# Seven block products with four shared sums, all on DVE, in a two-layer decoder on one core; norms by halves, a reordered start

## The chip, the cores and the metric

The kernel runs on one NeuronCore of a Trainium2 chip. The metric is device time in microseconds, from launch to end, as the median of several executions. PE is the matrix engine (TensorE), PEld its weight loads, DVE the VectorE, ACT the ScalarE, POOL the GpSimd engine and SP the SyncE, which here only issues transfers. All data are float32.

## What is computed

The input x holds 16 sequences of 128 tokens, 256 features each. It goes through two decoder layers of three parts; each part's output is added to x and the sum is layer-normed:

```python
x = layernorm(x + L0_attn(x))      # causal, 16 heads of 64
x = layernorm(x + L0_xattn(x))     # 8 experts of 512, relu, gated by token ids and ctx
x = layernorm(x + L0_ffn(x))       # 2 shared and 16 routed experts, top 2, silu
x = layernorm(x + L1_attn(x))      # 16 heads of 16, a band of 8 tokens to each side
x = layernorm(x + L1_xattn(x))     # 16 heads of 16, keys and values from ctx
x = layernorm(x + L1_ffn(x))       # 8 experts of 512, gelu, all of them, one factor per token
```

The two parts with eight dense experts (the second and the sixth) need, for every expert, `h = act(x @ up)` (512 wide) and `h @ down` (back to 256), summed over the experts.

## The kernel before

**Tiling.** The 16 sequences are four groups of four, 512 tokens each. A group's x stays in SBUF as 128 tokens by 4 sequences by 256 features, and its transpose xT as 2 x 128 features by 512 tokens. There are six parts for each of four groups, so 24 pieces of work, `run(number, g)`.

**Order of the work.** `Weaver` (from L196) is a planner inside the kernel: every part is a generator that emits instructions and yields how many microseconds of PE they are thought to take, or a time until which it wants to wait. `weave` takes pieces from a main stream (attention parts) and a side stream (`dense`: the expert parts) in given shares, and from short streams first (transposes, norms' tails, gates). At first only attention of groups 0 and 1 runs; then attention of groups 2 and 3 beside the dense parts of the first groups, and so on; the last group's sixth part runs alone at the end. The framework then orders each engine's instructions once more by a plan of its own, so the order in the built program differs from that of emission. Each engine's queue is worked off in order. An instruction that waits holds up all behind it on its engine.

**The start.** `load_x(0)`, the first quad of attention weights (four transfers of 256 KB: W_Q, W_K, W_V, W_O for four heads), then x of the other three groups (L106 to L108), all on SP's queue. Four streams `tail(-1, g)` transpose all groups' x (L51, copied by L244 and L246), and the first of them also starts `gates0`, which selects by token id in the transferred `it` and `cx` (L743, tile chose).

**attention0** (L347) goes through four quads of four heads. `project_quad` makes q and k (L288, drained by L361 and L366) and v (L305, L309); per quad and sequence follow scores (L382), mask, maximum and exponential (L319, L324, L329), the scaling of e by 1/sum on POOL (L335), its transpose (L51, drained by L344), the values (L424) and the output projection (L391). The next quad's projections are spread over the current quad's four sequences; the last quad has none to spread.

**products** (L640) does `h @ down` for an expert by Strassen's seven products of 2 x 2 blocks: tokens are halved, and h's features are halved. Of h, five sums of two blocks are needed (L663): three go to DVE and two to POOL, in tiles cm. Of the weights, seven combinations are made once on POOL (L629 to L631), used and written to HBM, from where later groups load them. The seven products of an expert are four calls of `multiply`, two products each (one in the last), in PSUM banks M of which there are two; DVE adds each bank to acc in SBUF (L681). After the eighth expert, `products_end` forms the four blocks of the result from the seven accumulated products with eight sums (L709 to L716, six on DVE and two on POOL, tile y), transposes them (L51), and adds them to x (L264 or L266). `Norm.done` (L274) then makes 1/sqrt(variance + eps) of four sequences, with the power on POOL (L278), and scales x (L280). For the last part, `store` writes a group's 512 KB of x out (L966). The hidden activations are drained by L774 (DVE, second part) or L933 (ACT, sixth part).

Of the kernel before, what the change touches and what calls it, by code (L numbers as in the profile page):

```python
# [8 lines left out]
F32 = mybir.dt.float32  # L9
# [18 lines left out]
def kernel(ctx: ExitStack, tc: tile.TileContext, a: dict, out: bass.AP):  # L28
# [77 lines left out]
    xs = [load_x(0)]  # L106
    first_quad = load_quad(0)
    xs += [load_x(g) for g in range(1, NG)]  # L108
# [5 lines left out]
    nc.gpsimd.memset(ones, 1.0)  # L114
    mhalf = cp.tile([P, GB], F32, tag="mhalf", name="mhalf")
# [133 lines left out]
    class Norm:  # L249
# [24 lines left out]
        def done(self):  # L274
            ve = sp.tile([P, GB], F32, tag="ve", name="ve")
            nc.vector.tensor_scalar(ve, self.mv[:, :, 1], EPS, None, ALU.add)
            rstd = sp.tile([P, GB], F32, tag="rstd", name="rstd")
            nc.gpsimd.tensor_tensor(rstd, ve, mhalf, ALU.pow)  # L278
            for b in range(GB):
                nc.vector.tensor_scalar(  # L280
                    self.x[:, b, :], self.x[:, b, :],
                    self.mv[:, b, 0:1], rstd[:, b:b + 1], ALU.subtract, ALU.mult,
                )
# [63 lines left out]
    def attention0(x, xT, g):  # L347
        norm = Norm(x)
        norm.bias(bo0)
        heads = {}  # L350

        def project_quad(j):
            wq, wk, wv, wo = first_quad if g == 0 and j == 0 else load_quad(j)
# [16 lines left out]
            heads[j] = qT, kT, v, wo  # L370

        def scores(j, b):
            qT, kT, _, _ = heads[j]
# [14 lines left out]
        def output(j, b, zT):  # L388
            po = bank("H")[:, :D]
            for i in range(2):  # L390
                mm(po, lhsT=zT[:, i, :], rhs=heads[j][3][:, i, :], start=i == 0, stop=i == 1)  # L391
            norm.add(b, po, last=j == 3)

        yield from project_quad(0)
        units = [(j, b) for j in range(4) for b in range(GB)]
        e, eT, zT, at = {}, {}, {}, {}
        for n in range(len(units) + 5):
# [17 lines left out]
            if m in eT:  # L415
# [5 lines left out]
                for i in range(2):  # L421
                    for k in range(2):
# [3 lines left out]
                            lhsT=heads[j][2][:, b, 64 * h:64 * h + 64], rhs=got[:, 2 * k + i, :],  # L426
# [9 lines left out]
            if n < 12:  # L436

                j, b = units[n]
                if b == 0:
                    ahead = project_quad(j + 1)  # L440
# [140 lines left out]
    def accumulate(hidden, down, n, us):  # L581
# [23 lines left out]
    PRODUCTS = (  # L605
        (((0, 0), None, None), ((0, 1), (1, 1), ALU.subtract)),
        (((1, 1), None, None), ((1, 0), (0, 0), ALU.subtract)),
        (((1, 0), (1, 1), ALU.add), ((0, 0), None, None)),
        (((0, 0), (0, 1), ALU.add), ((1, 1), None, None)),
        (((0, 0), (1, 1), ALU.add), ((0, 0), (1, 1), ALU.add)),  # L610
        (((1, 0), (0, 0), ALU.subtract), ((0, 0), (0, 1), ALU.add)),
        (((0, 1), (1, 1), ALU.subtract), ((1, 0), (1, 1), ALU.add)),
    )
# [3 lines left out]
    def load_blocks(layer, e, g, w):  # L617
# [6 lines left out]
        raw = raw.rearrange("p (q l) (j d) -> p q l j d", l=2, j=2)  # L624
        t = wp.tile([P, 7, 2 * P], F32, tag="down", name="wb0")
        blocks = t.rearrange("p s (q d) -> p s q d", q=2)
        for s, (_, (one, two, op)) in enumerate(PRODUCTS):
            if two is None:
                step = nc.gpsimd.tensor_copy(blocks[:, s], raw[:, :, one[0], one[1], :])  # L629
            else:  # L630
                step = nc.gpsimd.tensor_tensor(  # L631
                    blocks[:, s], raw[:, :, one[0], one[1], :], raw[:, :, two[0], two[1], :], op
                )
            if s == 0:
                together(step, *transposed_by[g])
        held = dp.tile([P, 7, 2 * P], F32, tag=f"wb{layer}", name="wbd", bufs=8)
# [4 lines left out]
    def products(load_up_of, blocks_of, hidden, finish):  # L641
# [6 lines left out]
        def half(e, at):  # L648
            return h[e].rearrange("p (q l) (i t) -> p q l i t", l=2, i=2)[:, :, at[1], at[0], :]

        def sums(e, phase):

            t = None
            for s in range(2 * phase, min(2 * phase + 2, 7)):
                one, two, op = PRODUCTS[s][0]
                if two is None:
                    parts[e, s] = half(e, one)
                    continue
                if t is None:
                    t = p3.tile([P, 2, 2, 2 * P], F32, tag="cm", name="cm")  # L660
# [427 lines left out]
```

## Time and profile before

| | us |
|---|---|
| median of 3 executions | 1839.93 (1838.93 to 1842.21) |
| the profiled execution | 1837.82 |
| its span, first to last instruction | 1836.1 |
| PE busy | 1757.7 (96%) |
| PEld busy | 1068.6 (58%) |
| DVE busy | 1050.7 (57%) |
| ACT busy | 731.0 (40%) |
| POOL busy | 673.8 (37%) |
| L663 on DVE, 192 instructions | 219.2 |
| L663 on POOL, 128 instructions | 205.3 |
| L335 on POOL, 128 instructions | 190.0 |

The granted clock of PE is 0.993 on average. All instruction times come from the one profiled execution. A timeline line gives start, length, engine, line of the kernel, operation, written tile `<-` read tiles, form, and count of the instructions merged into it; in square brackets stands how long the engine had been idle before it and what ended that wait. A PE record of 512 columns in float32 lasts 0.43 us start to start at full clock, one of 256 columns 0.22, a transpose of 128 columns 0.11; a float32 matmul is two records, a transpose one. A stage (from:to) is given in us from the start of the span.

### The profile page before, as it was taken

How to read it: one execution, taken by the hardware profiler on the slowest of the kernel's cores; microseconds unless marked ns; L12 is line 12 of the kernel's file. 1: busy time of each engine (PE TensorE's matmuls, PEld its weight loads, DVE VectorE, ACT ScalarE, POOL GpSimd, SP SyncE). 2: the span in 40 equal slices, each digit the busy share in tenths (PEclk: the TensorE clock that was granted, in tenths of full speed). 3: DMA queues.
4: the chain of work that ended last, by engine and by line, in shares of the span. 5: the costliest groups of instructions: out<-in, count | busy, mean ns of one | idle time of the engine just before them, and what ended most of it. 6: DMA issues, size and time to landing. Idle time of an engine off the chain costs nothing.

```text
span 1836.1 us, 21774 instructions
## 1 busy us (share of the span) xinstructions
PE 1757.7 (96%) x7602; PEld 1068.6 (58%) x7602; DVE 1050.7 (57%) x1927; ACT 731.0 (40%) x2161; POOL 673.8 (37%) x568
## 2 busy tenths in 40 slices
PE   7999999999999999999899999999898999999997
PEld 4655566666566565556556565556554565555664
DVE  3555655677565244676776853356546555645645
ACT  2434312112023452151340544936827548376221
POOL 5231235422131222353432624456554234344222
PEclk9999999999999999999999999999998999999999
DMA  5041223323321324123223214232232121222221
GB/s 170 24 134 46 87 78 126 124 75 122 121 86 46 111 92 138 61 99 111 75 87 98 82 57 121 70 116 97 79 116 75 63 94 65 75 75 84 106 96 51
DMA packets 73404, 166.69 MB, mean 91 GB/s; under 512 B 7000, under 2 KB 38800, under 8 KB 73296
## 3 DMA queue, kind: packets, MB, share of 16 engines
q1 hardware_dynamic: 70464, 150.17, 25.5%
q0 software_dynamic: 2832, 15.15, 2.0%
q8 instruction: 60, 0.98, 0.2%
q14 instruction: 48, 0.39, 0.1%
HBM read 148.32 MB, written 16.97 MB: 90 GB/s over the span
## 4 chain that ended last, share of the span: by engine, by line
PE 74%; DVE 11%; ACT 8%; issue 3%; POOL 2%; DMA 2%; SPq 0%; POOLq 0%; DVEq 0%; ACTq 0%
PE psH L288 33%; PE psM L671 16%; ACT e L329 4%; PE psH L305 4%; PE psM L592 4%; PE psO L51 4%; PE psH L391 3%; DVE cm L663 3%; PE psS L382 2%; PE psS L465 2%; PE psO L424 2%; PE psO L477 2%; DVE nmax L324 1%; PE psH L51 1%; ACT L933 1%
## 5 line engine op out<-in xcount | busy, mean ns | idle before, releaser
L288 PE MATMUL psH<-xT,we 128*128 128x512 f32 x1024 | 488.6, 599 | 5.6 <-ACT h L933 3.6
L335 POOL TENSOR_TENSOR e<-e,inv 128x512 f32<-128x512 f32 (+1 forms) x128 | 190.0, 1484 | 420.2 <-DVE inv L334 376.4
L663 POOL TENSOR_TENSOR cm<-h 128x512 f32<-128x512 f32 x128 | 205.3, 1621 | 356.1 <-DVE h L774 164.6
L671 PE MATMUL psM<-cm,wb 128*128 128x256 f32 x1280 | 313.9, 385 | 2.1 <-DVE acc L681 1.6
L329 ACT ACTIVATE e<-e,nmax 128x128 f32<-128x128 f32 x512 | 198.6, 389 | 258.6 <-DVE nmax L324 258.2
L671 PEld LDWEIGHTS psM<-cm,wb 128*128 128x128 f32 x1280 | 238.5, 190 | 99.3 <-issue 65.4
L288 PEld LDWEIGHTS psH<-xT,we 128*128 128x128 f32 x1024 | 187.4, 190 | 165.9 <-issue 137.1
L663 DVE TENSOR_TENSOR cm<-h 128x512 f32<-128x512 f32 x192 | 219.2, 1165 | 40.3 <-ACT h L933 37.9
L681 DVE TENSOR_TENSOR acc<-psM,acc 128x512 f32<-128x512 f32 x224 | 138.5, 619 | 174.8 <-PE psM L671 174.2
L344 ACT COPY eT<-psO 128x512 f32<-128x512 f32 x192 | 106.7, 586 | 147.2 <-PE psO L51 146.3
L933 ACT ACTIVATE h<-psH,b 128x512 f32<-128x512 f32 x128 | 87.2, 687 | 186.1 <-PE psH L288 169.3
L774 DVE SCALAR_TENSOR_TENSOR h<-psH,gt 128x512 f32<-128x512 f32 x128 | 87.7, 685 | 80.4 <-PE psH L288 80.3
L671 PE MATMUL psM<-h,wb 128*128 128x256 f32 x512 | 124.3, 385 | 0.0
L288 PE MATMUL psH<-xT,wquad 128*128 128x512 f32 x256 | 118.7, 606 | 4.6 <-DMA wquad<-in_L_attn_W_Q 1.6
L671 PEld LDWEIGHTS psM<-h,wb 128*128 128x128 f32 x512 | 96.5, 192 | 32.8 <-issue 18.7
L288 PE MATMUL psH<-xT,wg 128*128 128x512 f32 x256 | 115.5, 594 | 0.0
L51 PEld LDWEIGHTS psO<-ident,e 128*128 128x128 f32 x768 | 87.3, 141 | 48.4 <-issue 29.5
L51 PE MATMUL psO<-ident,e 128*128 128x128 f32 x768 | 112.5, 280 | 1.7 <-POOL e L335 0.9
L329 ACT ACTIVATE e<-psS,nmax 128x128 f32<-128x128 f32 x256 | 89.9, 377 | 38.4 <-DVE nmax L324 35.4
L329 ACT ACTIVATION_READ_ACCUMULATOR e<-e,nmax 128x1 f32 x512 | 95.7, 187 | 0.0
L457 POOL TENSOR_TENSOR kb<-kT,hm 128x512 f32<-128x512 f32 x64 | 70.1, 1097 | 69.2 <-PE psS L465 33.2
L879 POOL TENSOR_TENSOR hT<-sg,cw 128x512 f32<-128x512 f32 x32 | 41.4, 1292 | 130.6 <-DVE sg L878 130.6
(173 smaller groups left out, 2243.8 us busy)
## 6 DMA issues: line engine op xcount, KB each, us to landing
wb<-wbd SPq DMA_DIRECT2D x48, 896.0 KB
we<-in_L_xattn_proj_in SPq DMA_DIRECT2D x32, 512.0 KB
we<-in_L_ffn_w SPq DMA_DIRECT2D x32, 512.0 KB
wbd<-wb POOLq DMA_DIRECT2D x16, 896.0 KB, 6.0
gt<-gatesd SPq DMA_DIRECT2D x32, 256.0 KB
cw<-combd SPq DMA_DIRECT2D x64, 128.0 KB
wquad<-in_L_attn_W_Q SPq DMA_DIRECT2D x16, 256.0 KB
wquad<-in_L_attn_W_K SPq DMA_DIRECT2D x16, 256.0 KB
```

Source lines behind the costliest of these rows:

```text
L51: return nc.tensor.transpose(out_, in_, ident[:n, :n])
L288: mm(pt, lhsT=w[:, c, cols], rhs=xT[:, c, :], start=c == 0, stop=c == KC - 1)
L305: mm(pv[:, i, :], lhsT=xT[:, c, (b + i) * P:(b + i + 1) * P], rhs=w[:, c, :], start=c == 0, stop=c == k - 1,)
L329: nc.scalar.activation(e[:, h, :], s[:, h // (n // 2), h % (n // 2), :], AF.Exp, bias=nmax[:, h:h + 1], accum_out=total[:, h:h + 1],)
L335: nc.gpsimd.tensor_tensor(e, e, inv.unsqueeze(2).to_broadcast([P, n, P]), ALU.mult)
L344: return eT, nc.scalar.copy(eT, pt)
L592: step = mm(acc[b], lhsT=held[:, b * P:(b + 1) * P], rhs=down(i), start=i == 0 and b % 2 == 0, stop=i == n - 1, skip_group_check=True,)
L663: engine.tensor_tensor(t[:, s % 2], half(e, one), half(e, two), op)
L671: step = mm(pm[:, s % 2, :], lhsT=blocks[e][:, s, q, :], rhs=parts[e, s][:, q, :], start=q == 0 and s % 2 == 0, stop=q == 1, skip_group_ch ...
L681: nc.vector.tensor_tensor(to, pm[:, :len(slots), :], to, ALU.add)
L774: nc.vector.scalar_tensor_tensor(out=h, in0=ph, scalar=0.0, in1=up[1], op0=ALU.max, op1=ALU.mult)
L933: nc.scalar.activation(h, ph, AF.Gelu, bias=b1[:, 4 * e + c:4 * e + c + 1])
```

## The change

It has five parts.

1. *Start.* x of the first group and the first two quads are loaded first; the other groups' x are loaded and transposed in streams that begin at planned times 20, 40 and 60 us (`begin`). Nine matmuls of a tile of ones by itself are put ahead of everything on PE.
2. *attention0.* The projections of the next group's first quad are emitted during this group's last quad; what they make is kept in `heads0`, outside of the part.
3. *Sums.* Another form of the seven products: of h, four sums, two of them taken from an earlier one, all on DVE; of the weights, four differences and three copies. The order of slots in acc is m1, m2, m4, m7, m5, m6, m3.
4. *End of products.* The seven sums of the result begin while the last `multiply` still runs; the last product of the last expert isn't added to acc, but taken from its PSUM bank by the last sum.
5. *Halves.* `products_end` transposes and adds two sequences, norms them (`done(first, n)`), and stores them (256 KB) or goes on, then the other two.

The built program has 9 matmuls more on PE; on DVE 256 instead of 192 sums of h, 16 sums of y from acc fewer and 8 from PSUM more, 8 drains of acc fewer, and 16 + 16 instead of 24 instructions for variance + eps; on POOL no sums of h, 64 sums and 48 copies for weight blocks (80 and 32 before), 24 sums of y (16 before) and 32 powers (24 before); on SP 8 stores instead of 4.

```diff
-    xs = [load_x(0)]
-    first_quad = load_quad(0)
-    xs += [load_x(g) for g in range(1, NG)]
+    xs = [load_x(0)] + [None] * (NG - 1)
+    first_quads = [load_quad(j) for j in range(2)]
...
+    pw = bank("M")
+    for _ in range(9):
+        mm(pw[:, :P], lhsT=ones, rhs=ones, start=True, stop=True)
...
-        def done(self):
+        def done(self, first=0, n=GB):
+            at = slice(first, first + n)
             ve = sp.tile([P, GB], F32, tag="ve", name="ve")
-            nc.vector.tensor_scalar(ve, self.mv[:, :, 1], EPS, None, ALU.add)
+            nc.vector.tensor_scalar(ve[:, at], self.mv[:, at, 1], EPS, None, ALU.add)
...
-            nc.gpsimd.tensor_tensor(rstd, ve, mhalf, ALU.pow)
-            for b in range(GB):
+            nc.gpsimd.tensor_tensor(rstd[:, at], ve[:, at], mhalf[:, at], ALU.pow)
+            for b in range(first, first + n):
...
-        def project_quad(j):
-            wq, wk, wv, wo = first_quad if g == 0 and j == 0 else load_quad(j)
+        def project_quad(g, j):
+            wq, wk, wv, wo = first_quads[j] if g == 0 and j < 2 else load_quad(j)
+            xT = xTs[g]
...
-        yield from project_quad(0)
+        if (g, 0) not in heads0:
+            yield from project_quad(g, 0)
...
-            if n < 12:
+            if n < 16 and (n < 12 or g + 1 < NG):
                 j, b = units[n]
                 if b == 0:
-                    ahead = project_quad(j + 1)
+                    ahead = project_quad(g, j + 1) if j < 3 else project_quad(g + 1, 0)
...
+        minus = [(4, b01, b00), (5, b11, blocks[:, 4]), (2, blocks[:, 5], b10), (3, b11, b01)]
+        for s, one, two in minus:
+            step = nc.gpsimd.tensor_tensor(blocks[:, s], one, two, ALU.subtract)
+            if s == 4:
                 together(step, *transposed_by[g])
+        for s, one in ((0, b00), (1, b10), (6, b11)):
+            nc.gpsimd.tensor_copy(blocks[:, s], one)
...
+        def sums(e):
+            a00, a01, a10, a11 = (
+                h[e].rearrange("p (q l) (i t) -> p q l i t", l=2, i=2)[:, :, l, i, :]
+                for i in range(2) for l in range(2)
+            )
+            early = p3.tile([P, 2, 2, 2 * P], F32, tag="cm", name="cm")
+            late = p3.tile([P, 2, 2, 2 * P], F32, tag="cm", name="cm")
+            s3, s4, s1, s2 = early[:, 0], early[:, 1], late[:, 0], late[:, 1]
+            nc.vector.tensor_tensor(s3, a00, a10, ALU.subtract)
+            nc.vector.tensor_tensor(s1, a10, a11, ALU.add)
+            nc.vector.tensor_tensor(s2, s1, a00, ALU.subtract)
+            nc.vector.tensor_tensor(s4, a01, s2, ALU.subtract)
+            parts[e] = a00, a01, a11, s3, s1, s2, s4
...
+            if (e, phase) == (7, 3):
+                return pm[:, 0, :]
...
+                if e == 8 and c == 2:
+                    t = p3.tile([P, 2, 2, 2 * P], F32, tag="cm", name="y")
+                    m1, m2, m4, m7, m5, m6, m3 = (acc[:, s, :] for s in range(7))
+                    c00, c01, c10, c11 = t[:, 0, 0], t[:, 1, 0], t[:, 0, 1], t[:, 1, 1]
+                    nc.vector.tensor_tensor(c11, m1, m6, ALU.add)
+                    nc.gpsimd.tensor_tensor(c01, c11, m5, ALU.add)
+                    nc.vector.tensor_tensor(c10, c11, m7, ALU.add)
+                    nc.vector.tensor_tensor(c11, c10, m5, ALU.add)
+                    nc.vector.tensor_tensor(c10, c10, m4, ALU.subtract)
+                    nc.gpsimd.tensor_tensor(c01, c01, m3, ALU.add)
+                    nc.gpsimd.tensor_tensor(c00, m1, m2, ALU.add)
+        nc.vector.tensor_tensor(c01, last, c01, ALU.add)
+        finish(t)
...
+        yield UNTIL, weaver.now + 2.5
+        for i in (1, 0):
             pt = bank("H").rearrange("p (b d) -> p b d", b=2)
...
+            done(norm, 2 * i)
             yield 0.5
-        norm.done()
...
+    def store(norm, g, b):
+        norm.done(b, 2)
+        at = g * GB + b
         nc.sync.dma_start(
+            out=out[at:at + 2].rearrange("b p d -> p b d"), in_=norm.x[:, b:b + 2, :]
+        )
...
+    def begin(g):
+        if g > 0:
+            yield UNTIL, 20.0 * g
+            xs[g] = load_x(g)
+            yield UNTIL, 20.0 * g + 10.0
+        yield from tail(-1, g)
+
+    weaver.short += [Stream(begin(g)) for g in range(NG)]
```

## The prediction

> **What bounds the kernel now.** I read the page's busy shares first, then the busy times by stage, then the timelines of those stages in which the matrix engine idles.
>
> ```profile
> PE 1757.7 (96%) x7602; PEld 1068.6 (58%) x7602; DVE 1050.7 (57%) x1927; ACT 731.0 (40%) x2161; POOL 673.8 (37%) x568
> ...
> 0.00:10.00 10.00, 1.94 (x8) 1.57 (x8) 0.83 (x3) 1.87 (x2) 8.51 (x27) 1.00 0.81 232
> 10.00:20.00 10.00, 7.16 (x29) 4.86 (x30) 2.07 (x3) 1.76 (x3) 7.73 (x8) 1.00 1.08 310
> 140.00:200.00 60.00, 55.78 (x344) 35.87 (x343) 36.41 (x72) 29.15 (x113) 12.47 (x12) 0.97 0.15 47
> 800.00:1100.00 300.00, 288.41 (x1271) 175.57 (x1270) 209.31 (x390) 107.83 (x408) 117.08 (x77) 0.99 0.27 86
> 1200.00:1500.00 300.00, 282.90 (x1155) 168.71 (x1154) 165.24 (x285) 166.41 (x415) 149.06 (x138) 0.98 0.27 92
> 1800.00:1836.00 36.00, 23.67 (x91) 16.09 (x89) 20.08 (x39) 3.44 (x5) 9.56 (x7) 0.90 0.12 40
> ```
>
> (From the second line on: the stage, its length, busy us of PE, PEld, DVE, ACT and POOL, then granted clock, DMA share, GB/s.) PE is the bound: it is busy 1757.7 of 1836.1 us, and its work hardly changes. So the change is worth what it closes of 78.4 us of PE idle: 10.9 in the first 20 us, 9.9 in 20:200, 12.3 in the last 36, and 45 between, of which the stages 800:1100 and 1200:1500 hold 28.7. To this come stretches at half clock: 0.97 over 60 us is one of 3.4 us, 1.7 lost; the clock record has four more, at 910, 1395 and 1412 (two), 6.8 us.
>
> **1. The start:** order of loads, nine filler matmuls, the first group's transposes alone.
>
> ```profile
> 14.16 1.94 PE L51 MATMUL psH<-ident,x 128*128 128x128 f32 x8 [0.23 <-DMA x<-in_x]
> 16.63 1.07 PE L51 MATMUL psH<-ident,x 128*128 128x128 f32 x8 [0.53 <-DMA x<-in_x]
> 18.05 7.13 PE L288 MATMUL psH<-xT,wquad 128*128 128x512 f32 x16 [0.35 <-DVE xT L244]
> ...
> 25.55 0.69 DVE L743 SCALAR_TENSOR_TENSOR chose<-it,cx 128x512 f32<-128x512 int32 x1 [4.73 <-DMA cx<-in_ctx]
> ...
> 39.81 0.65 PE L51 MATMUL psO<-ident,e 128*128 128x128 f32 x4
> ```
>
> PE does all four groups' transposes before its first projection at 18.05, though the first group's xT is written at 7.64 (ACT's copy, 7.06 + 0.58) and its first two weights are in at 5.7 and 6.9 (landing records). Without the other groups PE starts at 7.6, 10.4 sooner. But what is late next? In the built order of the changed kernel DVE has its first L743, which waits for it and cx, ahead of the copy of v; the same 5 MB lie ahead of cx on SP's queue, so it still lands near 25.5. PE runs to 7.6 + 7.13 (projections) + 3.72 (v, L305) + 0.7 (scores) = 19.2 and then has no free bank until L743 and the copy are done: 25.55 + 2 x 0.69 = 26.9. From 25.55, eight DVE instructions (three more L743, two copies of v, mask, maximum, the first L743) at 0.65 go to 30.7, four exponentials 1.9, the reciprocal 0.2, POOL's e 1.04, some 0.4 of waits between: the first e is transposed near 34.3 instead of 39.81, 5.5 won. (POOL's weight blocks stand before that e; raw lands at 28 and they end by 30.5.)
>
> Against it, the other groups' 24 transposes move from idle time into a stretch where PE is busy: 24 x 1.07/8 = 3.2 us. And the stall of 7.7 us cools the array. [...] the 0.97 in 140:200, with a wait of 3.4 us at 144.62, agrees. So the warmth of the fillers (nine x 0.43 = 3.8 us, idle time, before x lands at 4.95) is lost again at 26.9: 1.7 (0 to 3.4). [...] eight took 1.94 and, after nothing but transposes, 1.07. [...] by the rows the transposes do it too; the stall overtakes either. Sum of the start: -5.5 + 3.2 + 1.7 = **-0.6** (-4 to +3).
>
> **2. The next group's first quad under this one's last.** The ends of attention0 had no projections to fill with; PE's waits over 0.13 us add to 3.2 us in 91:127, 3.4 in 193:232, 1.0 in 295:330, such as
>
> ```profile
> 113.52 3.70 PE L288 MATMUL psH<-xT,wquad 128*128 128x512 f32 x8 [1.18 <-DVE qT L361]
> ```
>
> Its four weight DMAs are issued earlier on SP and wait there for the buffer of the quad three before, as the last quad's do now (0.35 us of PE at 71.42). Of 7.6 us I take **-5.5** (-7.6 to 0). PE's wait at 144.62, for the second group's cx, stays: it is still queued behind gatesd and gt.
>
> **3. Four sums instead of five, all on DVE.** POOL loses its 128 L663 (205.3 us), DVE gets 64 more (192 to 256). The 1792 records of products stay.
>
> ```profile
> L663 DVE TENSOR_TENSOR cm<-h x192: 659/1126/2379, 225.5 to 1818.3; 128x512 f32<-128x512 f32 x192
> ...
> L663 DVE TENSOR_TENSOR cm<-h x3: 693/1425/1749, 1816.0 to 1818.3; 128x512 f32<-128x512 f32 x3
> ...
> L663 POOL TENSOR_TENSOR cm<-h x2: 1712/1745/1778, 1816.0 to 1817.8; 128x512 f32<-128x512 f32 x2
> ```
>
> (ns, shortest/median/longest; the whole run, then the last expert.) Alone a sum takes 0.69 on DVE, beside POOL's up to 1.75. By this row 256 sums cost 177 us, 42 less than the 219 now. [...] POOL keeps 673.8 - 205.3 = 468 us of other work, a quarter of the span, in pieces of 1.04 to 1.9 (a sum of y, 0.42 alone, took 2.12 beside e). [...] a quarter of the sums wait some 0.9 us, 0.69 + 0.23 = 0.92 each, 235 us, 16 more. I take the middle, DVE unchanged; either way it lies under PE, as DVE is 70% busy where it is fullest (800:1100). What PE can gain is shorter queues: six waits on DVE's h (L774) in 200:830 add to 4.6 us, six on eT, e and the exponentials in 1050:1625 to 6.7. The weight blocks' POOL work (16 times one sum of 0.83 becomes a copy of 0.37) is 7 us less, off the path.
>
> **4. Layers' ends.** y's sums begin an accumulation earlier, the last product skips acc, norms go by halves.
>
> ```profile
> 898.91 0.66 PE L51 MATMUL psH<-ident,y 128*128 128x128 f32 x4 [2.15 <-DVE y L712]
> 909.09 0.65 PE L51 MATMUL psH<-ident,x 128*128 128x128 f32 x2 [2.70 <-DVE x L280]
> ...
> 1394.38 1.65 PE L51 MATMUL psH<-ident,y 128*128 128x128 f32 x8 [2.54 <-DVE y L712]
> ```
>
> 7.4 us, and the half clock behind 909 and 1394, 3.4. Price: 8 more small DVE instructions (0.17) and 8 more powers on POOL (1.02), 10 us under PE; behind a power on POOL is the woven attention's e, 1 us later inside its planned 9 to 16. A new wait: y's last sum on DVE needs three POOL instructions (0.97 + 2 x 0.72), which can stand behind an e of 1.9; behind it on DVE are h and the masks, up to 2 us at 8 ends, 0 to +16. Of 22.1 us under 3 and 4 (4.6 + 6.7 + 7.4 + 3.4) I take half, **-11** (-22 to +10).
>
> **5. Switches of the array's shape.** In the trace a matmul on another part of the array than the one before (L382 to L51, L288 to L465) starts 0.095 later than one on the same. The built order has 584 such switches, not 551: **+3.1**.
>
> **6. The tail.**
>
> ```profile
> 1820.70 2.86 PE L671 MATMUL psM<-cm,wb 128*128 128x256 f32 x12 [1.19 <-DVE acc L681]
> ...
> 1831.73 0.39 SPq L966 DMA_DIRECT2D out<-x  x1
> ```
>
> 28 matmul records of 0.217 from 1815.9, without the 1.19, end at 1822. The ready half is transposed at 1823.4; its DVE rows (two adds, statistics, 1.7 in all) with y's last sum end at 1826.2, the other half's at 1828; then ve and power 1.2 and two scalings 0.7: last store at 1830.1 instead of 1831.7, and of 256 KB instead of 512, 0.8 shorter at the 310 GB/s of 10:20. **-2.5** (-4.5 to 0).
>
> **Sum.** -0.6 - 5.5 - 11 + 3.1 - 2.5 = -16.5 against the profiled execution (1837.82: its span and 1.7 around it), 1821.3. That execution is 2.1 under the runs' median of 1839.93; from the median, **1823**.
>
> **Rivals.** (a) The waits under 3 and 4 stay, others taking their place at the same two banks: -5.5 alone, 1834. For it: they are many and small, and PE hardly ever waited for POOL's L663 (0.5 us). Against it: DVE, which it does wait for, loses neighbours of 1.7 us. (b) All of 3 and 4 goes, and cx lands early: -22 - 4 - 7 + 3 - 4 = -34, 1806. (c) Slower: the lock. s1, s2 and s4 hang on one another on DVE, and in the woven stages each can find POOL in an e of 1.9. [...] If PE then waits out one lock in every fourth of 48 woven experts, that is 23 us, with the -5.5 of the rest 1857. Against it: 0.92 is estimated, not 2.
>
> **How the numbers follow.** Likeliest 0.52 (own range 1812 to 1834), (a) 0.20, (b) 0.13, (c) 0.15. 0.2% is 3.7 us, about what a measurement here can tell. Faster: the likeliest, (b) and nearly half of (a), 0.74; same: the rest of (a), 0.11; slower: (c), 0.15. 8 in 10: from the middle of (b), 1806, to where (c) begins, 1843.
>
> **What would show it.** First L288 near 7.6, then PE idle from 19 to 27 on DVE, which waits for cx; no waits over 0.5 at attention0's ends; L663 near 0.9 and POOL near 470 us; y and x waits under 1 us; the last store some 4 us before the end. I am wrong if cx lands earlier, if DVE's sums average over 1.3, or if the new order opens waits in the woven stages that the old one had not.

## The result, and the profile after

The changed kernel takes 1846.24 us (median of 20 executions, 1840.4 to 1850.55), the kernel before beside it 1837.12 (20, 1833.39 to 1842.21). The ratio is 1.0046, 95% interval 1.0038 to 1.0055: slower by 0.46%. Forecast were 1823, and faster. The profiled execution took 1843.18, its span is 1841.5.

First the page's busy shares and the busy times by stage, which answer to those shown of before:

```profile
PE 1770.8 (96%) x7620; PEld 1074.5 (58%) x7620; DVE 1017.5 (55%) x1983; ACT 724.2 (39%) x2155; POOL 476.1 (26%) x456
...
0.00:10.00 10.00, 8.45 (x35) 6.30 (x36) 1.58 (x4) 1.87 (x2) 8.52 (x27) 1.00 0.78 214
10.00:20.00 10.00, 7.56 (x33) 4.76 (x31) 0.75 (x1) 1.37 (x2) 5.01 (x6) 1.00 1.08 326
20.00:40.00 20.00, 13.89 (x46) 6.99 (x48) 9.68 (x17) 6.16 (x24) 4.29 (x6) 0.74 0.36 121
140.00:200.00 60.00, 57.28 (x313) 34.30 (x312) 31.68 (x63) 26.21 (x95) 13.97 (x16) 1.00 0.24 78
800.00:1100.00 300.00, 291.44 (x1235) 176.93 (x1236) 199.89 (x396) 92.12 (x344) 74.68 (x55) 0.99 0.28 92
1200.00:1500.00 300.00, 280.09 (x1109) 164.48 (x1109) 158.74 (x286) 172.52 (x457) 116.93 (x120) 0.97 0.26 87
1800.00:1841.00 41.00, 29.49 (x110) 20.57 (x108) 18.56 (x41) 4.81 (x7) 4.05 (x5) 0.87 0.10 36
```

PE is busier in 140:200 (57.3, was 55.8) and in 800:1100 (291.4, was 288.4), as forecast; in 1200:1500 it is less busy (280.1, was 282.9) at a lower clock (0.97, was 0.98). POOL fell to 476 us (about 470 forecast) and DVE by 33 us. The sums of h, two of the four lines, each from the view of its own source line:

```profile
L658 DVE TENSOR_TENSOR cm<-h x64: 641/691/1444, 230.2 to 1817.9; 128x512 f32<-128x512 f32 x64
...
L661 DVE TENSOR_TENSOR cm<-h,cm x64: 633/691/1412, 234.0 to 1823.0; 128x512 f32<-128x512 f32 x64
```

256 sums take 198 us, 0.77 each, where 0.69 (none held up) and, by estimate, 0.92 (a quarter held up by 0.9 us) were weighed. 73 of them overlap a POOL instruction and take 0.99 on average; the others take 0.69. Of the 73, 42 began while a POOL instruction had over 0.1 us left: each of these ended 0.55 us after the end of one on POOL (1.41 us in all, where a kb had 0.86 left). The other 31 took 0.63 to 0.69. These hold-ups are the lock of rival (c), so it is there, but DVE has 33 us less to do all the same, and the new sums alone, measured below, are a gain: they are not what made the kernel slower.

The start, PE's timeline (what follows 16.84 is the stall):

```profile
1.21 3.89 PE L117 MATMUL psM<-ones 128*128 128x128 f32 x18 [1.21 <-POOL ones L113]
4.93 1.05 PE L51 MATMUL psH<-ident,x 128*128 128x128 f32 x8
6.33 7.13 PE L292 MATMUL psH<-xT,wquad 128*128 128x512 f32 x16 [0.35 <-DVE xT L247]
...
16.84 0.71 PE L389 MATMUL psS<-kT,qT 64*128 64x128 f32 x8
26.11 6.57 PE L292 MATMUL psH<-xT,wquad 128*128 128x512 f32 x8 [8.55 <-DVE v L313]
...
37.53 0.66 PE L51 MATMUL psO<-ident,e 128*128 128x128 f32 x4
```

and on DVE, what it waited for:

```profile
24.76 0.69 DVE L742 SCALAR_TENSOR_TENSOR chose<-it,cx 128x512 f32<-128x512 int32 x1 [12.23 <-DMA cx<-in_ctx]
```

The copy of v, next on DVE's queue, starts at 25.37, behind this selection, and ends 0.06 us before PE goes on. The stall came where it was forecast and for the reason forecast. (One thing stated ahead of the prediction is inexact: the stream that transposes x does not start the gates. They are emitted behind attention0, and the framework's own plan lifts their selections up to here, in both kernels.)

**Where the time went.** I laid the two traces side by side at equal amounts of PE work (columns, weighted by the part of the array in use). In the times of the kernel before, the changed one is 8 us ahead at 148 us, 10 at 566, 14 at 929, 16 at 1062. That is as much as was forecast for the whole. Then it is 9 ahead at 1228 and 7 behind at 1287, 2 ahead at 1476 and 9 behind at 1660, and ends 5.4 behind (1841.5 against 1836.1). So the question is what happens in layer 1.

A second difference stands in the same trace. The scores of layer 1's two attention parts, attention1 and cross1, all groups (PE, tile psS), first of the kernel before, then of the changed one; the first of them are attention1's of group 0:

```profile
L465 PE MATMUL psS<-kb,qT x256: 589/664/1219, 771.8 to 1668.5; 64*128 64x512 f32 x128
```

```profile
L473 PE MATMUL psS<-kb,qT x256: 589/664/1191, 738.8 to 1654.5; 64*128 64x512 f32 x128
```

Layer 1's attention starts 33 us sooner (738.8, was 771.8), though the kernel is only some 10 us ahead. The attention stream has moved against the dense stream. The reason is in the planner's accounts. attention0 yields 82.2 us of planned PE time for a group: four quads at 10.3, and 41 for the rest. The overlap from group 1 to group 2 takes one quad out of the second weave (groups 2 and 3) and puts it into the first, where nothing is woven. The second weave gives dense 150 for each 81 of attention, so dense gets 10.3 x 150/81 = 19 us less before attention1 begins. The traces agree: dense matmuls of 314.8 us (at 0.43 for 512 columns) stand ahead of attention1's first scores, 334.5 in the kernel before, 19.7 less. The kernel's lead makes up most of the rest of the 33.

I call this the alignment, and count it on ACT's queue as built: how many drains of the third part (40 in all) and then of the sixth part (32 a group) stand before the first k of attention1 of group 2, cross1 of group 2, attention1 of group 3, cross1 of group 3. Before: 41, 67, 89, 113. Changed: 38, 61, 82, 106. At 40 the dense stream passes from the third part to the sixth.

### The profile page after: what moved, and what is told of

It reads as the page before. It is cut to its first block, busy times and chain, and to the rows that moved or that the text cites. A ratio compares the mean times of both kernels' runs of the same rounds, so it can differ in the third digit from the quotient of the medians.

```text
span 1841.5 us, 21636 instructions
## 1 busy us (share of the span) xinstructions
PE 1770.8 (96%) x7620; PEld 1074.5 (58%) x7620; DVE 1017.5 (55%) x1983; ACT 724.2 (39%) x2155; POOL 476.1 (26%) x456
## 4 chain that ended last, share of the span: by engine, by line
PE 78%; DVE 7%; ACT 7%; DMA 3%; POOL 2%; issue 2%; SPq 0%; POOLq 0%; DVEq 0%; ACTq 0%
PE psH L292 34%; PE psM L670 19%; PE psH L309 4%; PE psO L51 4%; ACT e L333 4%; PE psM L600 3%; PE psH L398 3%; PE psS L473 2%; PE psS L389 2%; PE psO L432 2%; PE psO L485 1%; PE psH L51 1%; DVE nmax L328 1%; ACT L333 1%; DMA wquad<-in_L_attn_W_Q 1%
## 5 line engine op out<-in xcount | busy, mean ns | idle before, releaser
L670 PE MATMUL psM<-cm,wb 128*128 128x256 f32 x1024 | 267.1, 385 | 1.3 <-DVE acc L682 1.3
L670 PEld LDWEIGHTS psM<-cm,wb 128*128 128x128 f32 x1024 | 191.8, 191 | 69.5 <-issue 44.5
L682 DVE TENSOR_TENSOR acc<-psM,acc 128x512 f32<-128x512 f32 (+1 forms) x216 | 135.6, 628 | 168.6 <-PE psM L670 167.9
L670 PE MATMUL psM<-h,wb 128*128 128x256 f32 x768 | 202.9, 387 | 0.0
L670 PEld LDWEIGHTS psM<-h,wb 128*128 128x128 f32 x768 | 142.9, 192 | 56.1 <-issue 35.5
L473 PE MATMUL psS<-kb,qT 64*128 64x512 f32 x256 | 82.0, 644 | 14.1 <-ACT e L333 5.0
L292 PEld LDWEIGHTS psH<-xT,wquad 128*128 128x128 f32 x256 | 47.5, 194 | 67.2 <-issue 47.2
L328 DVE TENSOR_REDUCE nmax<-e 128x4 f32<-128x512 f32 (+1 forms) x96 | 82.5, 859 | 2.0
```

Source lines behind the costliest of these rows:

```text
L292: mm(pt, lhsT=w[:, c, cols], rhs=xT[:, c, :], start=c == 0, stop=c == KC - 1)
L328: nc.vector.tensor_reduce(nmax.rearrange("p (s h) -> p s h", s=2), s, AX.X, ALU.max, negate=True)
L473: mm(s[:, k, :], lhsT=qT[rows, c, at], rhs=kb[rows].rearrange("p h k -> p (h k)"), start=True, stop=True,)
L670: step = mm(pm[:, s % 2, :], lhsT=blocks[e][:, s, q, :], rhs=parts[e][s][:, q, :], start=q == 0 and s % 2 == 0, stop=q == 1, skip_group_ch ...
L682: nc.vector.tensor_tensor(to, pm[:, :len(slots), :], to, ALU.add)
```

## The experiments

Theory P: this alignment makes the loss. Rival F: the new form of the products and the halves cost by themselves where they meet layer 1's attention.

**Restore the alignment, or spoil it.** Share of the second weave, in the changed kernel and in the kernel before:

```diff
-    weaver.weave(Stream(chain((0, 2), (0, 3))), dense, (81.0, 150.0))
+    weaver.weave(Stream(chain((0, 2), (0, 3))), dense, (74.0, 150.0))   # after_share74
+    weaver.weave(Stream(chain((0, 2), (0, 3))), dense, (86.4, 150.0))   # before_share86
```

> One number is changed in the changed kernel: the share of the attention stream in the second weave is 74 instead of 81 (the dense stream keeps 150). By the overlap the attention of groups 2 and 3 has one quad of projections less to hand to that weave (10.3 us of planned time), so the planner has given the dense stream less by the time attention1 begins, and in all of layer 1 attention runs ahead of where it stood in the kernel before. With 74 the built order has attention1 and cross1 of groups 2 and 3 begin beside the same dense expert as in the kernel before. Theory P (the loss in the second half is this alignment): the 22 us lost after 1062 us mostly come back, 1846 - 18 = 1828, between 1822 and 1834. Rival F (the loss is the price of the products' new form and of the halves, wherever they meet attention16): 1843 to 1849, as the changed kernel. In between: both.

Measured: 1834.68, ratio to before 0.9987 (0.9976 to 0.9998). 11.6 us came back, fewer than 18, and the time lies 0.7 above theory P's range. New waits take a part of it: in 850 to 1107 PE's waits over 0.3 us add to 14.0 us, 9.3 in the changed kernel.

> The mirror of the last: the kernel before with a share of 86.4 instead of 81 in the second weave, so that attention1 and cross1 begin beside the same experts as in the changed kernel, and nothing else is changed. Theory P: the kernel before loses what the changed one lost in the second half, 1837 + 10 to 22 = 1847 to 1859. Rival F: 1835 to 1840, as before.

Measured: 1849.05, ratio 1.0059 (1.0046 to 1.0072). One number makes the kernel before slower by 11.5 us, with nothing of the change in it.

**The overlap out, and alone.** after_no_overlap (the changed kernel):

```diff
-            if n < 16 and (n < 12 or g + 1 < NG):
+            if n < 12:
...
-                    ahead = project_quad(g, j + 1) if j < 3 else project_quad(g + 1, 0)
+                    ahead = project_quad(g, j + 1)
```

before_overlap is the kernel before with heads0 and the lines that the first diff takes away.

> The changed kernel without the overlap alone: the next group's first quad is projected when that group begins, as before; this also gives attention1 the alignment of the kernel before. Theory P: loses the overlap's gain (5.5 by the prediction) and wins back the second half (about 18): 1846 + 5 - 18 = 1833, between 1827 and 1839. Rival F: 1846 + 5 = 1851, between 1848 and 1854.

Measured: 1829.75, ratio 0.9953 (0.9941 to 0.9965).

> The overlap alone put into the kernel before (Strassen's five sums, whole norms, the old start). Theory P: wins 5.5 at the ends of attention0 and loses in the second half by the new alignment, 1837 - 5 + 10 to 22 = 1842 to 1854. Rival F: 1837 - 5.5 = 1832.

Measured: 1842.1, ratio 1.0028 (1.0017 to 1.0039). All four speak for theory P: the first lies just above its range, the last at the lower edge, none within 8 us of what rival F says. after_share74 keeps the overlap with its early loads and its held tiles, so these are not what costs. Without the overlap the change is a gain of 8 us.

**Which of the three overlaps.** Those from group 0 to 1 and 2 to 3 stay within one weave; that from 1 to 2 crosses the border.

```diff
-            if n < 16 and (n < 12 or g + 1 < NG):
+            if n < 16 and (n < 12 or g in (0, 2)):   # after_inner_overlap
+            if n < 16 and (n < 12 or g == 1):        # after_border_overlap
```

> The changed kernel with the overlap only from group 0 to 1 and from group 2 to 3. These two stay within one weave each, so no planned work leaves the second weave and layer 1 keeps the alignment of the kernel before. Theory P (only the overlap from group 1 to 2, which crosses the border between two weaves, does harm, by the alignment): 1829.8 - 2/3 of 5.5 = 1826, between 1823 and 1829. Rival O (the overlap itself is no gain in the changed kernel, as the comparison of the share of 74 with no overlap, 1834.7 against 1829.8, could be read): 1830 to 1836.

Measured: 1830.58, ratio 0.996 (0.9948 to 0.9971): no harm, but no gain over 1829.75 either. At equal work it is some 3 us ahead of after_no_overlap at 130 us (the end of the first attention0), 1.7 at 202, and 0.6 or less from 520 on.

> The other half: the changed kernel with the overlap from group 1 to 2 alone. Theory P: the whole loss of the alignment and a third of the gain, 1829.8 - 2 + 12 to 14 = 1840 to 1842 or a little more, up to 1848. Rival O: 1830 to 1834.

Measured: 1848.39, ratio 1.0053 (1.0037 to 1.0069), just above the upper end. The whole loss sits in the overlap that crosses the border. At equal work this kernel is first ahead of after_no_overlap, by 8 us at 900 and 10 at 1060, then 12 behind at 1300 and 19 at 1700. So the shift wins before it loses, and about 9 of the changed kernel's lead of 16 us at 1062 go with the overlap.

**The products alone** (before_products: the kernel before with parts 3 and 4 of the change, norms and store whole):

> The new form of the seven products alone, put into the kernel before: four sums on DVE, four differences and three copies for the weight blocks, the early sums of y, the last product taken from its bank. Start, attention0, whole norms and the whole store stay, and so does the alignment of layer 1. The prediction's part 3 and most of part 4 and 5: -11 + 3 = 1829, between 1824 and 1834. Rival (a): the waits stay under other names, 1836 to 1839. Rival F (the new form costs in layer 1): 1840 to 1850.

Measured: 1830.21, ratio 0.9961 (0.9946 to 0.9976). The size fits; the place doesn't, so that it fits is in good part luck. Of the 9.4 us between the two spans, some 6 are won by 293 us, and before 225 us no sum of h runs. What is gone is a wait of PE in the kernel before, with the half clock behind it:

```profile
144.62 0.71 PE L382 MATMUL psS<-kT,qT 64*128 64x128 f32 x8 [3.37 <-DVE e L319]
```

DVE's timeline shows why, the kernel before first:

```profile
143.21 0.69 DVE L743 SCALAR_TENSOR_TENSOR chose<-it,cx 128x512 f32<-128x512 int32 x1 [4.19 <-DMA cx<-in_ctx]
...
143.91 0.66 DVE L319 TENSOR_TENSOR e<-psS,causal 128x512 f32<-128x512 f32 x1
```

```profile
140.89 0.68 DVE L319 TENSOR_TENSOR e<-psS,causal 128x512 f32<-128x512 f32 x1
143.56 0.69 DVE L734 SCALAR_TENSOR_TENSOR chose<-it,cx 128x512 f32<-128x512 int32 x1 [1.99 <-DMA cx<-in_ctx]
```

DVE still waits for the same ctx, but the framework's plan now has the scores' mask ahead of the waiting selection, and PE goes on.

**The halves alone, and the start alone:**

> The halves alone, put into the kernel before: norms of two sequences at a time, and two stores of 256 KB for each group. The prediction's tail: the store is half as long and the first half is scaled while the second is still added: -1 to -2 at the end, and 0 to -4 at layers' ends, 1835. If a power on POOL behind the old sums and weight blocks holds up x twice instead of once: 1839 to 1842.

Measured: 1835.12, ratio 0.9984 (0.9977 to 0.9991), as expected.

> The new start alone, put into the kernel before: x of the first group and two quads first, the nine filler matmuls, x of the other groups at planned times. The prediction's part 1, -0.6. As the changed kernel stood 1.0 us behind at the end of its first 77 us: +1, 1838.5, between 1836 and 1841; but if the order of the second group's gates (the wait of 3.5 us at 144 in the kernel before) is as fickle as it looks, this wait may go too: 1833.

Measured: 1841.52, ratio 1.0015 (1.0007 to 1.0023), 2.8 us slower by the ratio and just above the expected range; its profiled execution stands only 0.3 behind, so no trace shows where the rest goes.

**The start's stall taken away** (on after_inner_overlap):

```diff
+                if g == 0:
+                    together(step, *transposed_by[0])   # chose waits for the group's later transpose
```

> The last but one (overlap inside the weaves), and in it the eight selections of the first group's gates (chose) wait for the first group's second transpose, about 110 us later, so that DVE doesn't stand at the start for the ctx that lands at 24.7. Everything is still computed. Theory of the start (PE's 8.7 us and the half clock of 10.2 us behind it come from this one wait): the first e is transposed near 29 instead of 37.5, and the time is 6 to 10 us under the overlap inside the weaves, so about 1818. Rival: PE, freed there, waits at the same banks for what lands next (x of the second group, the third quad), or the gates, now late, hold up the second group's ctx near 145 to 165: 0 to 3 us under it.

Measured: 1829.02, ratio 0.9957 (0.9941 to 0.9973), 1.6 us under after_inner_overlap: the rival was right. PE's timeline of it:

```profile
32.02 1.12 PE L51 MATMUL psO<-ident,e 128*128 128x128 f32 x4 [5.77 <-POOL e L339]
...
140.19 0.66 PE L51 MATMUL psO<-ident,e 128*128 128x128 f32 x4 [2.69 <-POOL e L339]
```

The first e is transposed at 32.0 instead of 37.5, and at 77 us the kernel is 3.9 ahead. But PE then waits at the start for the softmax itself, and the gates, moved to 130 to 145, meet the second group there: by 202 us the lead is gone.

**How the time goes with the alignment.** third62 and third66 change the share of the third weave of the changed kernel, all else kept; the others change the second weave's share.

```diff
-    weaver.weave(Stream(chain((3, 0), (4, 0), (3, 1), (4, 1))), dense, (68.0, 150.0))
+    weaver.weave(Stream(chain((3, 0), (4, 0), (3, 1), (4, 1))), dense, (62.0, 150.0))   # after_third62
+    weaver.weave(Stream(chain((3, 0), (4, 0), (3, 1), (4, 1))), dense, (66.0, 150.0))   # after_third66
```

> The changed kernel, all of its parts and all three overlaps, with one number changed: the share of attention in the third weave is 62 instead of 68. Up to the third weave its order is that of the changed kernel (attention of groups 0 and 1 in layer 1 still runs ahead), but attention1 of group 2 begins again beside the first hidden block of the sixth part, as in the kernel before, and so all that follows. Theory P in its narrow form (the harm is done where attention1 of group 2 meets the change from the third part to the sixth, and where cross1 of group 3 meets the change of groups two pieces later): the 12.7 and 10.3 us that PE stood more in these two stages come back, 4 to 5 of them given up after 1637 us: 1846 - 18 = 1828, between 1824 and 1832. If the harm is in the alignment from 742 us on: 1836 to 1848.

Measured: 1829.10, ratio 0.9955 (0.9941 to 0.9969): theory P in its narrow form.

> The new products alone (1830.2) with a share of 85 instead of 81 in the second weave: attention1 of group 2 begins one hidden block ahead of the sixth part (39 of 40) instead of one behind it (41), cross1 of group 3 at 109 instead of 113. If the harm is a collision with the change of parts: most of it is there already, 1838 to 1846. If time grows evenly with the shift (38 costs 12 to 17): about two thirds, 1838 to 1841, and the two stages would not stand out. If only the shift of the changed kernel hits it: 1829 to 1832.

Measured: 1817.83, ratio 0.9893 (0.9879 to 0.9906). None of the three guesses: one block ahead of the change of parts is not bad but 12 us better than one block behind it. So I asked whether this holds for the changed kernel too, and how far the good place reaches.

> The changed kernel, all parts, with a share of 66 in the third weave instead of 68: attention1 and cross1 of groups 2 and 3 begin at hidden blocks 39, 62, 84 and 109, exactly as in the new products with a share of 85 (1817.8), and one to three blocks later than in the changed kernel (38, 61, 82, 106). If the time of the second half follows from the alignment alone: 1817 to 1821, 26 us under the changed kernel by two units of one share. If the changed kernel's other parts (start, overlap, halves) add waits there: 1824 to 1846.

Measured: 1812.66, ratio 0.9863 (0.9845 to 0.9881). One share moved by 2 of 68 makes the changed kernel 33.6 us faster, and 25 faster than the kernel before, better than either guess. This version beats both.

> The last, and a share of 62 instead of 68 in the fourth weave: the first alignment stays (39), the later ones move to 65, 89 and 115, about those of the kernel before (67, 89, 113), where the change of parts near 1550 us costs 14 to 16 us of PE's time instead of 25. Theory: 10 us less in that stage, about 5 given up in the next: 1811 to 1817. If what is won comes back elsewhere: 1817 to 1825.

 

(Also the fourth weave's share, 62 for 68.) Measured: 1834.77, ratio 0.998 (0.9972 to 0.9989). Missed: the stage meant to gain (1474 to 1637 in the table below) has 13.8 us of PE's waits where after_third66 has 13.3, and the two around it have 11.7 and 15.0 where 4.1 and 4.6 stood.

> The new products alone with a share of 76: attention1 of group 2 begins at hidden block 45 (41 with 81), cross1 at 70, the others at 91 and 116. If only a narrow collision just ahead of the change of parts does harm: 1826 to 1832, as with 81. If the time rises the further attention runs behind: 1835 to 1842.

Measured: 1828.49, ratio 0.9948 (0.9933 to 0.9962), as with 81.

> The new products alone with a share of 91: blocks 34, 55, 76 and 101, further ahead than in the changed kernel (38). If the collision is narrow: 1818 to 1828. If running ahead does harm from 38 on: 1842 or more.

Measured: 1834.67, ratio 0.9985 (0.9977 to 0.9993), between the two guesses. And the kernel before at the good place:

> The kernel before, none of the change, with a share of 85 in the second weave: blocks 39, 62, 84 and 109, as in the well aligned changed kernel (1812.7) and the new products (1817.8). If alignment acts alike on old and new products: 1837.5 - 12 = 1825.5, and the whole change is worth 13 us at equal alignment. If the old sums on POOL, which lies under the same POOL queue, spoil the good alignment: 1830 to 1845. If the old kernel gains as much as 20: the change is worth no more than 5.

Measured: 1843.56, ratio 1.0031 (1.002 to 1.0042). The second guess: the old form does not find the good place. Together, medians in us (the other three blocks move along with the first):

| attention1 of group 2 begins at block | old products | new products alone | changed kernel |
|---|---|---|---|
| 34 | | 1834.67 | |
| 38 | 1849.05 | | 1846.24 |
| 39 | 1843.56 | 1817.83 | 1812.66 |
| 41 | 1837.5 | 1830.21 | 1829.10 (third62) |
| 45 | | 1828.49 | |

At block 41 the change is worth 8 us, at 38 it is worth 3, at 39 it is worth 31. Parts and alignment do not add. Kernels with the same products and the same four blocks lie near each other: with the new products at 41 the six measured take 1829.0 to 1834.7, at 38 the changed kernel and after_border_overlap 1846.2 and 1848.4 (after_power_first below, which changes an order at that place, aside); with the old ones at 38 before_overlap and before_share86 1842.1 and 1849.1.

**What is so dear at 38.** For this I took from each PE record the time to the next start, less its length at full clock (0.43 for 512 columns), and summed what is over 0.3 us, by stages that end at the middle expert of a group. Half clock is in it, switches and small waits are not. (The 12.7 and 10.3 us in the expectation of after_third62 count these too.)

| stage (us in the kernel before) | before | changed | no overlap | third66 | power first |
|---|---|---|---|---|---|
| 0 to 293 | 22.9 | 16.2 | 20.5 | 16.5 | 15.6 |
| 293 to 977 | 18.7 | 8.7 | 15.0 | 9.1 | 9.1 |
| 977 to 1301 | 12.6 | 21.8 | 11.5 | 4.2 | 16.7 |
| 1301 to 1474 | 14.5 | 11.8 | 10.8 | 4.1 | 11.4 |
| 1474 to 1637 | 4.6 | 13.3 | 4.0 | 13.3 | 13.4 |
| 1637 to the end | 6.5 | 4.5 | 7.1 | 4.6 | 4.5 |

Up to 977 us the changed kernel has 16.7 us fewer of these waits than the kernel before; 10.6 of them go with the overlap (4.3 and 6.3 in the two stages). Then it has 9 more in each of two stages. The first holds the change from the third part to the sixth. PE's timeline there, of the changed kernel:

```profile
1228.50 1.13 PE L473 MATMUL psS<-kb,qT 64*128 64x512 f32 x4
1232.16 1.89 PE L51 MATMUL psH<-ident,x 128*128 128x128 f32 x8 [2.53 <-DVE x L284]
1235.99 2.04 PE L473 MATMUL psS<-kb,qT 64*128 64x512 f32 x2 [1.94 <-DVE e L323]
1237.96 3.10 PE L292 MATMUL psH<-xT,we 128*128 128x512 f32 x4
```

In the kernel before attention1's projections (tile wa) still lie between x's transposes and fill such waits:

```profile
1230.88 0.60 PE L51 MATMUL psH<-ident,x 128*128 128x128 f32 x4
1231.41 1.13 PE L465 MATMUL psS<-kb,qT 64*128 64x512 f32 x4
1232.87 0.65 PE L51 MATMUL psH<-ident,x 128*128 128x128 f32 x4 [0.33 <-DVE xT L244]
1234.05 1.98 PE L288 MATMUL psH<-xT,wa 128*128 128x512 f32 x4 [0.53 <-ACT h L933]
```

Who is late? In the changed kernel POOL's queue:

```profile
1224.09 1.41 POOL L632 TENSOR_TENSOR wb<-raw 128x256 f32<-128x256 f32 x2 [4.42 <-DMA raw<-in_L_ffn_w]
...
1228.80 1.05 POOL L282 TENSOR_TENSOR rstd<-ve,mhalf 128x4 f32<-128x4 f32 x1
1229.83 2.03 POOL L465 TENSOR_TENSOR kb<-kT,hm 128x512 f32<-128x512 f32 x2
```

The variance is ready at 1224.8. But a weight block, for whose raw weights POOL waited until 1224.1, stands ahead of the power, which runs at 1228.8. So x is scaled from 1229.9 to 1233, and PE's transposes wait 2.5 us; the next scores then find their one bank undrained (1.94 us). Behind the first of these waits the granted clock is 0.50 from 1233.4 to 1240.2. after_power_first changes this one order:

```diff
+            if (layer, e) == (1, 1):
+                together(step, power[0])     # each step of this weight block waits for the power
```

> The changed kernel as it is (shares 81 and 68, blocks 38, 61, 82, 106); the second weight block of the sixth part, which POOL makes at 1224 us ahead of the power of group 3's norm, has to wait for this power. In the built order the power then stands first, and attention's kb ahead of the block too. In the trace of the changed kernel ve is ready at 1224.8, the power runs at 1228.8, PE waits 2.5 us for x and then 1.9 for a score bank, and the clock goes to half for 6.8 us. Theory M (this one order on POOL is the head of the loss in the stage 977 to 1301, 12.7 us): 1846 - 6 to 12 = 1834 to 1840. Rival N (the scores of attention1 have no projections beside them there, and wait for banks and the softmax whatever POOL does first): 1843 to 1847.

Measured: 1837.12, ratio 0.9992 (0.9983 to 1.0): 9 us back in the medians, 6.7 between the spans of the two profiled executions: theory M. POOL's queue in it:

```profile
1224.51 1.03 POOL L284 TENSOR_TENSOR rstd<-ve,mhalf 128x4 f32<-128x4 f32 x1 [5.03 <-DVE ve L282]
```

(One kb of attention1 also moves up, into the weight block, so this is the power's order and a little more.) The busy times of the stretch, changed kernel, then power first, then third66 (its own stretch around the change of parts):

```profile
1215.00:1245.00 30.00, 25.53 (x81) 13.38 (x80) 16.68 (x30) 15.66 (x44) 17.70 (x23) 0.89 0.40 132
```

```profile
1215.00:1245.00 30.00, 27.45 (x93) 13.88 (x92) 19.78 (x33) 18.57 (x45) 20.43 (x23) 1.00 0.40 132
```

```profile
1205.00:1235.00 30.00, 29.98 (x97) 16.23 (x95) 19.85 (x36) 15.58 (x43) 20.29 (x22) 1.00 0.36 132
```

PE's busy time goes from 25.5 of 30 us at a clock of 0.89 to 27.5 and then 30.0 at full clock. So the late power is the head of the loss in this stage: in the table, 5.1 of the 10.3 us by which the changed kernel exceeds the one without overlap. The other half is the place itself. Why block 39 is so good to the new products and not to the old (6.0 us of such waits fewer up to 293, 10.6 fewer in 293 to 977, 6.1 in 977 to 1301, 1.7 in the next stage), and what costs 9 us in 1474 to 1637 in both the changed kernel and third66, was not tried.

## Why the prediction was wrong

The step that failed is the second, "the next group's first quad under this one's last". It was costed by the waits it fills, -5.5, and by its DMAs. It was never asked what it takes out of the planner's accounts. The edit takes a quad of planned work across the border of two weaves, so attention1 meets the dense stream 3 to 7 blocks earlier. The price, net of all that it wins, is what after_border_overlap shows: 1848.4 against 1829.8 without overlap, 18.6 us. The last paragraph of the prediction names the sign of it ("if the new order opens waits in the woven stages that the old one had not"), but no rival had its price. That the shift is a loss is in part luck: it ends at block 38, and at 39 the same change is the fastest kernel measured here.

Point by point:

| step | forecast | measured |
|---|---|---|
| 1. start | -0.6 (-4 to +3) | +0.9 by 77 us in the trace, +2.8 alone |
| 2. overlap, its own gain | -5.5 (-7.6 to 0) | -1.7 after the first end, nothing left in the median (inner overlap) |
| 2. overlap, alignment | not in the sum | +18.6 net |
| 3, 4. sums and layers' ends | -11 (-22 to +10) | -8 (products alone), but some 6 of 9.4 at the start; halves -3; PE's waits for y and x 8.7, were 8.8 |
| 5. switches | +3.1 | +2.9 (575 switches in the trace, were 544, 0.094 each) |
| 6. tail | -2.5 (-4.5 to 0) | 0.0 (5.4 behind at equal work at 1769 us, 5.4 at the end) |

*Start.* The chain to the stall's end was right (26.1; forecast 26.9). Behind it, e is ready at 32.8, but on PE two sets of projections and two of scores stand ahead of its transpose, which the forecast didn't count; by my estimate (37.5 less the 2.9 of half clock below) they would end at 34.6 at full clock, about where it put the transpose. The clock's term was too small: it stays at half from 21.7 to 31.9, PE is at work there from 26.1, so 5.8 us at half speed cost 2.9, not 1.7. The fillers do their work, as forecast: the clock record goes to full at 4.6 us, and the first eight transposes take 1.05, were 1.94. In the kernel before, it goes to full at 16.3 us, when PE had run nothing but transposes: there these were enough, as the prediction's rows said (eight in 1.94, later in 1.07). "PE's wait at 144.62 stays" was wrong: it hung on one order in DVE's plan. The kernels with the new products or the overlap from group 0 to 1 lost it; with the old products and no overlap (the start alone, the halves alone, the shares of 85 and 86.4) it stayed at 3.2 to 4.0 us.

*Sums.* 0.77 lay nearer to no lock: the estimate's share was about right (73 of 256 sums beside POOL), but each lost 0.3 us, not 0.9. At the old alignment the new form gains only some 3 us outside of the start, as rival (a) had it (other waits take the place). At block 39 old and new products, alike aligned, stand 25.7 us apart in their spans. So the term's size was not a number at all: it depends on where the streams meet.

*Layers' ends and the tail.* PE's waits for y and x add to 8.7 us, 8.8 in the kernel before: this part of the term gained nothing, and "y and x waits under 1 us" did not come. The new wait was named in part 4 and given "0 to +16". It is there at the end, the timeline of the last y:

```profile
1824.41 0.72 POOL L710 TENSOR_TENSOR y<-acc 128x256 f32<-128x256 f32 x1 [91.85 <-DVE acc L682]
...
1827.93 0.96 POOL L705 TENSOR_TENSOR y<-y,acc 128x256 f32<-128x256 f32 x1 [2.80 <-DVE y L704]
1828.92 0.43 DVE L707 TENSOR_TENSOR y<-y,acc 128x256 f32<-128x256 f32 x1 [0.61 <-POOL y L705]
1828.97 0.96 POOL L709 TENSOR_TENSOR y<-y,acc 128x256 f32<-128x256 f32 x1
1829.96 0.42 DVE L711 TENSOR_TENSOR y<-psM,y 128x256 f32<-128x256 f32 x1 [0.61 <-POOL y L709]
...
1830.78 1.97 PE L51 MATMUL psH<-ident,y 128*128 128x128 f32 x8 [3.25 <-DVE y L708]
```

and in the kernel before:

```profile
1824.94 1.34 PE L51 MATMUL psH<-ident,y 128*128 128x128 f32 x8 [1.38 <-DVE y L712]
```

Only one of the seven sums (L710) begins early. The first of the others needs the sixth slot, whose drain ends at 1827.4, and then DVE and POOL hand y to and fro. PE waits 3.25 us for y where it waited 1.38. From the end of the last product to the end of the span it is 14.0 us instead of 12.5 (1841.5 - 1827.53, 1836.1 - 1823.56), although the last store is shorter (3.1 us from its issue to the end of the span, 4.4 in the kernel before). The wait of 1.19 us ahead of the last products, which is gone as forecast, pays for this: the tail as a whole is neither longer nor shorter.

## What to carry to other kernels

Where a planner deals out two streams by shares, every edit that moves work across the border of a weave also moves all that comes after; count the planned time on both sides before costing the edit. Look for the places where one stream changes part: there a late weight block ahead of a small power on POOL's queue was worth 9 us, and about as much hung on what else lay beside it. Try each version at a few alignments before judging it: the worth of the change here went from 3 to 31 us with one share.

## What was not expected of the hardware

*How long the clock stays down.* Ahead of the two kernels' ends the clock record is at half for 3.41, 6.83 or 10.24 us at a time. A wait of 3.4 us on PE went with 3.4 us at half clock (the kernel before, 144 us), one of 2.5 with another of 1.9 soon behind it with 6.8 (the changed kernel, 1232 us), one of 8.6 with 10.2 (the changed kernel, 26 us). Behind one of 5.8 (inner_gates_later, 32 us) four transposes took 1.12 us, where they take 0.66 at full clock. Length isn't all: in the kernel before, a wait of 2.7 us (909) went with 3.4, one of 3.6 (1413) with 6.8. The prediction priced the stall at 1.7 us, one stretch of 3.4 at half clock. I counted PE's idle time in steps of 3.41 us from each change of the clock record, for the ten stretches at half clock that both kernels have ahead of their ends. In all ten the last step at half clock is busy from end to end, and no step of the stretch before it is. The step before the fall is idle from end to end in one alone; in the others it holds 1.8 to 2.8 us of idle time (2.0 for the fall behind the wait at 144.62).

*A short instruction beside POOL.* Of the four scalings of x at 1229.9 one took 2.13 us beside POOL's two kb, where the median of this line is 0.41. 91 of its 96 ran with POOL idle and none of them took over 0.42; of the five beside POOL three took 1.7 to 2.1. The prediction had two scalings at 0.7 us in all; this one lies on the path that stops PE, whose transposes wait 2.53 us for x.
